# Two attention layers on one core: v from seven block products instead of eight

## The chip, the core and the metric

The kernel runs on one core of a Trainium2 chip. A core has a matrix engine (TensorE, "PE" in the profile, with its weight loads as "PEld"), a vector engine (VectorE, "DVE"), a scalar engine (ScalarE, "ACT"), GpSimd ("POOL") and SyncE ("SP"). POOL and SP here mostly issue DMAs. TensorE writes only to PSUM, and VectorE and ScalarE take the results out. The metric is the device time of one execution in microseconds (us).

## The reference

The input x has 16 batches of 256 channels by 32 x 32 positions. Two layers are applied, each `x = x + attention(norm(x))`. Cut to what matters, a layer is:

```python
def layer(x):                                 # x: (16, 256, 32, 32)
    xf = group_norm(x, G=16).reshape(16, 256, 1024)
    q, k, v = (einsum('oc,bcn->bon', Wt, xf) + bt[None, :, None] for Wt, bt in ...)
    q, k, v = (y.reshape(16, 4, 64, 1024) for y in (q, k, v))     # 4 heads
    sim  = einsum('bhdi,bhdj->bhij', q, k)
    qpos = einsum('hdi,bhdj->bhij', (rel_h + rel_w), q)
    attn = softmax(sim + qpos, axis=-1)
    out  = einsum('bhdn,bhmn->bhdm', v, attn)
    return x + out.reshape(x.shape)
```

All data are float32. The normalisation takes its groups over the last axis, two columns of the 32 to a group. What the change touches is v: for each batch and layer, a 1024 x 256 matrix of tokens times a 256 x 256 weight.

## The kernel before

A **unit** is one batch in one layer. There are 32 units, in an order that puts units of layer 0 and of layer 1 beside each other (`units`). A unit has four **blocks**, (pr, half): pr is the pair of heads (0 or 1), half is the half of the 1024 query positions. They are called b0 to b3 here; n is the number of a block over all units, and `block(n)` writes it out. In a block:

- There are eight tiles of scores, j = 0 to 7, of 128 keys by two heads by 512 queries. `seed` (line 344) has VectorE write the position term into two banks of PSUM; `scores` (line 373) has TensorE add k times q, and ScalarE takes the exponential into a buffer p of the pool `ppool` (12 buffers).
- `add_up` (line 397) sums the p tiles on VectorE. The eighth is added by an accumulating DMA from POOL (`add_last`, line 435), and the sum over keys is folded by further DMAs from POOL and SP (`fold`, `stack_up`, `fold_again`, `fold_stack`, `spread_sums`). `reciprocals` (line 508) makes the denominators, and `finish` (line 551) multiplies by them and adds the residual, two VectorE operations for a pair of blocks, and for layer 1 a store on SP.
- `attend` (line 409) multiplies v by p on TensorE, in two halves; `take_out` copies the result with ScalarE.

TensorE works on four quarters of its array, 64 x 64 each. A product over 128 rows needs two of them, which add into the same bank, so every product is made in two halves (`stretches`, line 157; `BANKS`): in the first half each row half of the array has a bank of its own, in the second they change over. The second half may start when the first has ended. A small write on POOL, the token (`word`, line 164), carries this from TensorE to TensorE.

Between the score tiles of a block stand products for the next blocks (`prepare`, line 593): in b0 the second half of the tokens' v and q of the second pair; in b1 k and the position term of that pair; in b2 q and k of the next unit's first pair; in b3 the first half of the next unit's v, and its position term. `values` (line 286) makes v for 512 tokens: 32 matmuls of 256 columns. `norms` lays the group sums, squares and the application of the normalisation for later units over the blocks, on ScalarE (tables `APPLY`, `SUMS`, `SQUARES`).

PSUM has eight banks, used as four buffers of two (`ring`). Three serve the score tiles in turn; they and the fourth also serve the products above and the result of `attend`. A buffer can be written again when the copy or the exponential that reads it is done. The program runs under a manual schedule: each engine and each queue executes its instructions in the order in which the code above makes them, and the order within `block` is written by hand.

Of the kernel before, what the change touches and what calls it, by code (L numbers as in the profile page):

```python
# [9 lines left out]
F32 = mybir.dt.float32  # L10
F32R = mybir.dt.float32r
I32 = mybir.dt.int32
AF = mybir.ActivationFunctionType
ALU = mybir.AluOpType
# [3 lines left out]
P = 128  # L18
HALF = 512
G = 16  # L20
# [32 lines left out]
def fast_path(ctx, tc, sh, x, layers, out, W, den_all, token, good, flag):  # L53
# [36 lines left out]
    small = ctx.enter_context(tc.tile_pool(name="small", bufs=2))  # L90
    kqpool = ctx.enter_context(tc.tile_pool(name="kqpool", bufs=2))
    vpool = ctx.enter_context(tc.tile_pool(name="vpool", bufs=2))
    ppool = ctx.enter_context(tc.tile_pool(name="ppool", bufs=12))
    apool = ctx.enter_context(tc.tile_pool(name="apool", bufs=3))
    spool = ctx.enter_context(tc.tile_pool(name="spool", bufs=2))
    fpool = ctx.enter_context(tc.tile_pool(name="fpool", bufs=2))
# [52 lines left out]
    def psum2(tag, name):  # L149
        return ps_s.tile([P, 2, HALF], F32, tag=tag, name=name)  # L150
# [6 lines left out]
    def stretches(products):  # L157

        done = []

        def word():
            if len(done) == 1:
                done.append(nc.gpsimd.memset(token, 0.0).ins)  # L166
                tc.add_manual_dep(done[1], done[0].name, SYNC, reason="first stretch done")

        def of(t):
            if t == 1:  # L170
                word()
            for ins in products(t):
                if t == 0:
                    done[:] = [ins.ins]
                elif len(done) == 2:
                    tc.add_manual_dep(ins.ins, done.pop().name, SYNC, reason="second stretch")

        of.word = word
        return of
# [106 lines left out]
    def values(u, g, pv):  # L286
# [24 lines left out]

        return stretches(products), out_of_psum

    def positions(u, pr, pa):

        l = units[u][1]
        pa = pa.rearrange("p h (e r) -> p h e r", r=D)

        def products(t):
            if t == 1:  # L320
                return
            for j in range(NT):
                for rs, h in BANKS[0]:
                    for x, c in enumerate(QUARTERS):
                        j0 = j * P + x * D
                        yield nc.tensor.matmul(  # L326
                            pa[c, h, j, :],
                            qs[u, pr][rs, j0 : j0 + D],
                            W.rel[l][rs, pr, :],
                            start=(j == 0),  # L330
                            stop=(j == NT - 1),
                            skip_group_check=True,
                        )

        def out_of_psum():
            abt[u, pr] = kqpool.tile([P, 2, NT, D], F32, tag="abt", name=f"abt_{u}_{pr}")
            nc.scalar.copy(abt[u, pr], pa)

        return stretches(products), out_of_psum
# [33 lines left out]
    def scores(blk, j, tag=None):  # L373
# [20 lines left out]
        nc.scalar.activation(p, ps, AF.Exp, bias=W.shift)  # L394
        probs[blk, j] = p

    def add_up(blk, j):
        u, pr, half = blk
        if j == 0:
            return  # L400
        if j == 1:
            accs[blk] = apool.tile([P, 2, HALF], F32, tag="acc", name=f"acc_{u}_{pr}_{half}")
            nc.vector.tensor_tensor(accs[blk], probs[blk, 0], probs[blk, 1], ALU.add)  # L403
        else:
            nc.vector.tensor_tensor(accs[blk], accs[blk], probs[blk, j], ALU.add)  # L405
# [3 lines left out]
    def attend(blk, po):  # L409

        u, pr, half = blk

        def products(t):
            for j in range(NT):
                p = probs[blk, j]
                for rs, a in BANKS[t]:
                    for h, c in enumerate(QUARTERS):
                        c0 = pr * P + h * D
                        yield nc.tensor.matmul(  # L419
                            po[c, a, :QUART],  # L420
                            vts[u][rs, j, c0 : c0 + D],
                            p[rs, h, a * QUART : (a + 1) * QUART],
                            start=(t == 0 and j == 0),
                            stop=(t == 1 and j == NT - 1),
                            skip_group_check=True,
                        )

        return stretches(products)
# [20 lines left out]
    def stack_up(blk):  # L449

        u, pr, x = blk
        if x == 0:
            stacks[u, pr] = spool.tile([P, HALF], F32, tag="stack", name=f"stack_{u}_{pr}")
        for h, at in beside(blk):
            nc.sync.dma_start(at, accs[blk][:R, h, :])
# [108 lines left out]

    def in_range(den, i):

        t = fpool.tile([P, den.shape[-1]], F32, tag=f"range{i}", name=f"range{i}", bufs=1)
        yield nc.vector.tensor_scalar(t, den, DEN_LO, None, ALU.is_ge)
        yield nc.vector.scalar_tensor_tensor(t, den, DEN_HI, t, ALU.is_le, ALU.mult)
        yield nc.vector.tensor_reduce(good[:, i : i + 1], t, AX.X, ALU.min)  # L570
# [22 lines left out]
    def prepare(u, b):  # L593

        x, y = ring[3], ring[2]
        if b == 0:
            return (
                values(u, 1, psum2(x, f"pv_{u}_1")),
                project(u, 1, "q", psum2(y, f"pq_{u}_1")),
            )  # L600
        if b == 1:
            return (
                project(u, 1, "k", psum2(x, f"pk_{u}_1")),
                positions(u, 1, psum2(y, f"pa_{u}_1")),
            )
        u += 1
        if u == NU:
            return (nothing, nothing), (nothing, nothing)
        if b == 2:
            return (  # L610
                project(u, 0, "q", psum2(x, f"pq_{u}_0")),
                project(u, 0, "k", psum2(y, f"pk_{u}_0")),
            )
        return (
            values(u, 0, psum2(x, f"pv_{u}_0")),
            positions(u, 0, psum2(y, f"pa_{u}_0")),
        )


    APPLY = {0: (0, 1, 5, 9, 9), 1: (9, 9, 9, 11, G)}  # L620
    SUMS = {0: (0, 0, 0, 2, 9), 1: (9, 11, 12, G, G)}
    SQUARES = {2: (0, 0, 5, 11, G)}

    FIRST_SQUARES = {0: (3, 5, 9, G, G)}
# [15 lines left out]
    def block(n):  # L640
# [3 lines left out]

        stacked = blocks[n - 3][:2] if half == 1 and n > 2 else None
        summed = blocks[n - 4][:2] if half == 0 and n > 3 else None
        before = blocks[n - 5][:2] if half == 1 and n > 4 else None
        after = blocks[n + 1] if n + 1 < len(blocks) else None
        previous = blocks[n - 1] if n > 0 else None
        one, two = u + 1 < NU, u + 2 < NU  # L650
# [5 lines left out]
        folded = n - 1 < FOLDED  # L656
        if not pieces:
            return block_without_pieces(n, half)

        if previous:  # L660
            if half == 0:
                add_up(previous, 5)
            add_up(previous, 6)
            if folded:
                add_last(previous)
            else:
                add_up(previous, 7)
# [15 lines left out]
        first.word()  # L683
        if half == 0:
            second.word()
        if stacked:
            fold_stack(*stacked, D)
        if summed:
# [9 lines left out]
        scores(blk, 5)  # L698
        if previous and folded:
            stack_up(previous)  # L700
        add_up(blk, 2)
        if n == 0:
            reduced(2, 0)
# [18 lines left out]
        values_of_p = attend(blk, po)  # L722
        values_of_p(0)
        if two and half == 1:
            if b == 1:
                mean_out = norm_mean(u + 2, filled(f1, f"pm_{n}", 0.0))
            else:
                mean_out = norm_var(u + 2, filled(f1, f"pm_{n}", EPS / 2))
        if after:
            scores(after, 0)  # L730
        if n == 0:
            mean_out = norm_var(1, filled(f1, f"pm_{n}", EPS / 2))
        values_of_p.word()
        if stacked:
            fold_stack(*stacked, R // 2)
        if previous and folded:
# [2 lines left out]
            load_x(units[u + 3][0], range(pr_, pr_ + 1) if u > 0 else range(CC))  # L739
        if half == 0 or n == len(blocks) - 3:  # L740
            add_up(blk, 5)
        if before:
            finish(*before)
        if two and half == 1 or n == 0:
# [9 lines left out]
        if summed:  # L754
            reciprocals(*summed)
        norms(u, b, 3)
        values_of_p(1)
        take_out(blk, po)
        pos[n] = po
# [399 lines left out]
class Weights:  # L1159


    def __init__(self, tc, sh, layers, const):
        nc = tc.nc
        self.sh, self.layers = sh, layers

        def new(name, shape):
            return const.tile(shape, F32, tag=name, name=name)

        self.ident = new("ident", [P, P])
        make_identity(nc, self.ident)  # L1170
        self.avg, self.ones = new("avg", [P, P]), new("ones", [P, P])
        self.mhalf, self.shift = new("mhalf", [P, sh.H]), new("shift", [P, 1])
        for t, v in (
            (self.avg, 1.0 / sh.COUNT),
            (self.ones, 1.0),
            (self.mhalf, -0.5),
            (self.shift, -SHIFT),
        ):
            nc.vector.memset(t, v)
        both = range(len(layers))  # L1180
        self.wq, self.wk, self.wv = (
            [new(f"{n}{l}", [P, sh.CC, sh.C]) for l in both] for n in ("Wq", "Wk", "Wv")
        )
        self.bq, self.bk, self.bv = (
            [new(f"{n}{l}", [P, sh.CC]) for l in both] for n in ("bq", "bk", "bv")
        )

        self.rel = [new(f"rel{l}", [P, sh.CC, sh.D]) for l in both]

    def load_rest(self, queue, l):  # L1190

# [70 lines left out]
```

## Time and profile before

| what | value |
|---|---|
| median of 3 runs | 2531.03 us (2530.86 to 2531.93) |
| span of the profiled execution | 2529.2 us |
| TensorE busy | 2508.5 us, 99% |
| VectorE busy | 2270.3 us, 90% |
| ScalarE busy | 1945.5 us, 77% |
| GpSimd busy | 836.1 us, 33% |
| granted clock of TensorE, mean | 0.999 |
| DMA queue of POOL / of SP, share of 16 DMA engines | 31.5% / 11.9% |

The times below come from the one profiled execution. Lines of groups read: source line, engine, operation, output <- inputs by the program's names, shapes, count, then busy us and mean ns of one. A line of the timeline reads: start (us from the start of the span), duration (us), engine, source line, operation, tiles, shape, count, and in brackets how long the engine stood idle before it and whose end it waited for. A line of the chain reads: start, duration, engine, tile, line, count. A float32 matmul stands as two instructions in the trace, so x8 is four matmuls, one for each quarter of the array. The end of a matmul in the profile is modelled and overlaps the start of the next, so stretches of TensorE are measured here from start to start.

### The profile page before, as it was taken

Reading aid. Unit: us, or ns where it says so; the run is one execution under the profiler, and the core shown is the slowest. Engines: PE = TensorE matmul, PEld = TensorE weight load, DVE = VectorE, ACT = ScalarE, POOL = GpSimd, SP = SyncE. Lnnn points to the kernel's source line nnn. Section 1 sums busy time; section 2 is a strip of 40 time slices with the busy share of each in tenths; the row PEclk is TensorE's granted clock in tenths of the full one; section 3 lists DMA queues with packets and bytes.
Section 4 is the critical chain, followed back from the end, with each engine's and each line's share of the span. In section 5 each row is a group of like instructions: output and inputs, shape, how many; then the busy total and the mean of one; then the engine's idle time right before and its main releaser. Section 6 shows DMA issues by size and latency. Waiting matters only on the chain.

```text
span 2529.2 us, 85968 instructions
## 1 busy us (share of the span) xinstructions
PE 2508.5 (99%) x37472; PEld 1331.3 (53%) x37472; DVE 2270.3 (90%) x2143; ACT 1945.5 (77%) x3855; POOL 836.1 (33%) x1196
## 2 busy tenths in 40 slices
PE   8999999999999999999999999999999999999998
PEld 4555555555555555555555555555555555555554
DVE  7898998999989989999899899998998999989998
ACT  6778777788777787777877778877778777787754
POOL 1332333323333333333233332333323333323320
PEclk9999999999999999999999999999999999999999
DMA  3344444444445444444444444454454444444442
GB/s 93 75 81 83 77 87 76 95 95 93 99 88 103 80 84 93 90 83 96 94 85 95 81 97 80 84 106 88 89 111 82 87 81 84 78 83 80 95 82 70
DMA packets 119841, 221.58 MB, mean 88 GB/s; under 512 B 53912, under 2 KB 55448, under 8 KB 119456
## 3 DMA queue, kind: packets, MB, share of 16 engines
q0 software_dynamic: 53712, 130.10, 31.5%
q1 hardware_dynamic: 65744, 85.90, 11.9%
q8 instruction: 295, 4.83, 0.8%
q14 instruction: 90, 0.74, 0.1%
HBM read 51.78 MB, written 17.30 MB: 27 GB/s over the span
## 4 chain that ended last, share of the span: by engine, by line
PE 96%; DVE 2%; DMA 1%; issue 1%; POOL 0%; SPq 0%; ACT 0%; DVEq 0%; POOLq 0%
PE po L419 34%; PE ps L385 34%; PE pv L298 9%; PE pk L268 9%; PE pq L268 9%; PE pa L326 2%; DVE ps L349 1%; DVE acc L405 0%; PE pm L209 0%; DMA den_all<-d 0%; DMA stack<-stack 0%; DMA x<-in_x_dram 0%; DVE acc L403 0%; PE raw_t L126 0%; POOL rstd L237 0%
## 5 line engine op out<-in xcount | busy, mean ns | idle before, releaser
L349 DVE TENSOR_TENSOR ps<-abt 128x1024 f32<-128x1024 f32 x1018 | 1229.2, 1230 | 227.0 <-ACT p L394 142.9
L394 ACT ACTIVATE p<-ps,shift 128x1024 f32<-128x1024 f32 x1024 | 1091.3, 1114 | 332.6 <-PE ps L385 332.6
L385 PE MATMUL ps<-q,k 64*64 64x512 f32 x8192 | 986.2, 590 | 1.3 <-DVE ps L349 1.2
L419 PE MATMUL po<-p,v 64*64 64x256 f32 x16384 | 930.6, 376 | 0.0
L419 PEld LDWEIGHTS po<-p,v 64*64 64x64 f32 x16384 | 629.6, 133 | 363.1 <-issue 77.2
L405 DVE TENSOR_TENSOR acc<-acc,p 128x1024 f32<-128x1024 f32 x643 | 780.6, 1214 | 7.0
L385 PEld LDWEIGHTS ps<-q,k 64*64 64x64 f32 x8192 | 306.7, 133 | 397.8 <-issue 272.9
L166 POOL MEMSET token<- 1x1 f32 x320 | 36.4, 114 | 1042.8 <-PE po L419 463.2
L465 POOL DMA_DIRECT2D stack<-stack x310 | 254.9, 822 | 189.5 <-DMA stack<-stack 103.6
L298 PE MATMUL pv<-Wv,xn 64*64 64x256 f32 x4096 | 244.3, 376 | 0.4 <-POOL token L166 0.3
L268 PE MATMUL pk<-xn,Wk 64*64 64x512 f32 x2048 | 242.9, 590 | 0.0
L268 PE MATMUL pq<-xn,Wq 64*64 64x512 f32 x2048 | 242.9, 589 | 0.0
L460 POOL DMA_DIRECT2D stack<-acc x248 | 221.8, 1079 | 40.2 <-issue 31.7
L248 ACT ACTIVATE xn<-x,nshift,rstd 128x128 f32<-128x128 f32 x496 | 210.4, 497 | 1.1 <-POOL nshift L239 1.1
L298 PEld LDWEIGHTS pv<-Wv,xn 64*64 64x64 f32 x4096 | 153.8, 133 | 102.7 <-issue 51.5
L436 POOL DMA_DIRECT2D acc<-p x124 | 118.9, 958 | 247.6 <-ACT od L480 159.4
L190 ACT ACTIVATE junk<-x,neg 128x128 f32<-128x128 f32 x505 | 197.7, 400 | 0.0
L480 ACT COPY od<-po 128x512 f32<-128x512 f32 x127 | 74.3, 585 | 116.9 <-PE po L419 116.9
L403 DVE TENSOR_TENSOR acc<-p,p 128x1024 f32<-128x1024 f32 x128 | 155.8, 1217 | 0.0
L441 POOL DMA_DIRECT2D acc<-acc x124 | 105.9, 854 | 148.2 <-DMA acc<-p 137.9
L268 PEld LDWEIGHTS pq<-xn,Wq 64*64 64x64 f32 x2048 | 78.3, 133 | 141.0 <-issue 132.5
L190 ACT ACTIVATE junk<-x 128x128 f32<-128x128 f32 x464 | 140.6, 313 | 0.0
(78 smaller groups left out, 1122.9 us busy)
## 6 DMA issues: line engine op xcount, KB each, us to landing
acc<-p POOLq DMA_DIRECT2D x124, 512.0 KB, 5.7
rden<-rd SPq DMA_DIRECT2D x126, 256.0 KB, 5.8
acc<-acc POOLq DMA_DIRECT2D x124, 256.0 KB, 3.5
x<-in_x_dram SPq DMA_DIRECT2D x32, 512.0 KB, 3.9
stack<-acc SPq DMA_DIRECT2D x248, 64.0 KB, 2.1
stack<-acc POOLq DMA_DIRECT2D x248, 64.0 KB, 2.9
out_dram<-x SPq DMA_DIRECT2D x31, 512.0 KB, 3.7
stack<-stack POOLq DMA_DIRECT2D x62, 128.0 KB, 4.0
```

Of the source, the lines that this page charges most:

```text
L190: nc.scalar.activation(junk, grouped(xt[units[u][0]], g), func, accum_out=into[:, g : g + 1], **bias)
L248: nc.scalar.activation(grouped(xns[u], g), grouped(xt[units[u][0]], g), AF.Identity, bias=shift[:, g : g + 1], scale=rstd[:, g : g + 1],)
L268: yield nc.tensor.matmul(pk[c, nh, :], w[l][rs, cc, c0 : c0 + D], xns[u][rs, cc, nh * HALF : (nh + 1) * HALF], start=(t == 0 and cc == 0), ...
L298: yield nc.tensor.matmul(pv[c, a, i, :], xns[u][rs, cc, j0 : j0 + D], W.wv[l][rs, cc, :], start=(t == 0 and cc == 0 and i == 0), stop=(t = ...
L349: nc.vector.tensor_tensor(ps.rearrange("p h (w y) -> p h w y", y=H), ab[:, :, :H].unsqueeze(2).to_broadcast([P, 2, XH, H]), ab[:, :, H + h ...
L385: nc.tensor.matmul(ps[c, h, :], a[hs, j0 : j0 + D], b[hs, columns], start=bool(tag) and i == 0, stop=i == len(terms) - 1, skip_group_check ...
L394: nc.scalar.activation(p, ps, AF.Exp, bias=W.shift)
L403: nc.vector.tensor_tensor(accs[blk], probs[blk, 0], probs[blk, 1], ALU.add)
L405: nc.vector.tensor_tensor(accs[blk], accs[blk], probs[blk, j], ALU.add)
L419: yield nc.tensor.matmul(po[c, a, :QUART], vts[u][rs, j, c0 : c0 + D], p[rs, h, a * QUART : (a + 1) * QUART], start=(t == 0 and j == 0), s ...
L460: nc.gpsimd.dma_start(at, acc[R:D, h, :], accum_op=ALU.add)
L465: nc.gpsimd.dma_start(stack[:rows_], stack[rows_ : 2 * rows_], accum_op=ALU.add)
```

## The change

v of the next unit is no longer made with eight products of blocks (128 channels by 128 channels by 512 tokens) in b3 and b0, but with seven, all in b3, for all units but the first.

- **Sums of the inputs.** The 256 channels x 1024 tokens of the normalised x are four quarters. Three sums of them are made by DMA into a tile t: SP copies a quarter twice (`sum_copies`), POOL adds two quarters (`sum_additions`), SP copies a sum twice, POOL adds twice more. The copies and two of the additions stand in b2, the third addition in b3. `Weights.mix` makes the four sums of the weights, once per layer, on VectorE.
- **Products.** `Values.half` makes one row half of a product with eight matmuls of 128 columns; `stage` interleaves two such halves on different quarters of the array. Product 1 is paired with score tile 2, which is cut into 128 columns for it (`score_half`, `exponential`); products 6 and 2, 5 and 7, 3 and 4 make pairs. Bank 0 of the buffer `pw` holds a running sum that ScalarE copies into v four times (`keep`); bank 1 holds a second one that VectorE adds to or takes from v four times (`combine`). A pair that writes a bank waits for the keep or combine that reads it.
- **Order of the blocks.** `block_with_values` writes out b3, `block_with_q` b0 (from the second unit on), in which only q is left between score tiles: half of it ahead of tile 4, half after tile 5. `attend` in b3 is cut so that pair 4 stands within its first half. The addition of tile 5 moves from the end of b0 to the start of b1. The first pair's `finish` moves from b1 to b2, and the tables of `norms` are shifted a little.
- **Buffers.** `ppool` goes from 12 to 10 buffers, which makes room for t; a range check near the end takes a buffer of that pool.

```diff
-    ppool = ctx.enter_context(tc.tile_pool(name="ppool", bufs=12))
+    ppool = ctx.enter_context(tc.tile_pool(name="ppool", bufs=10))
+    tpool = ctx.enter_context(tc.tile_pool(name="tpool", bufs=1))
...
+        into, of = (t[:, 2:4, :], t[:, 0:1, :]) if second else (t[:, 0:2, :], x[:, 1:2, :])
+        nc.sync.dma_start(into, of.to_broadcast([P, 2, HALF]))
...
+        into, of = (
+            (t[:, 0:2, :], x[:, 0:4:3, :]),
+            (t[:, 2:4, :], x[:, 3:4, :].to_broadcast([P, 2, HALF])),
+            (t[:, 3, :], x[:, 2, :]),
+        )[i]
+        nc.gpsimd.dma_start(into, of, accum_op=ALU.add)
...
+        def half(self, i, rs, whole):
+            a, x, w, first = self.terms[i]
+            for part in range(4):
+                for q, c in enumerate(QUARTERS):
+                    j0 = part * P + q * D
+                    yield nc.tensor.matmul(
+                        self.pw[c, a, part * P : (part + 1) * P],
+                        x[rs, j0 : j0 + D],
+                        w[rs, :],
...
+            for _ in range(4):
+                for g in streams:
+                    for _ in range(2):
+                        made.append(next(g))
...
+        def keep(self, oc, nh, sign):
+            nc.scalar.activation(
+                self.out(oc, nh), by_token(self.pw[:, 0, :]), AF.Copy, scale=sign
+            )
+        def combine(self, oc, nh, op):
+            o = self.out(oc, nh)
+            nc.vector.tensor_tensor(o, o, by_token(self.pw[:, 1, :]), op)
...
-    SUMS = {0: (0, 0, 0, 2, 9), 1: (9, 11, 12, G, G)}
+    SUMS = {0: (0, 0, 0, 1, 7), 1: (7, 9, 11, G, G)}
...
+        if b == 2:
+            sum_copies(u + 1, False)
         if previous:
-            if half == 0:
+            if half == 0 or u > 0:
                 add_up(previous, 5)
...
+    def block_with_q(n):
...
+        for j in range(1, 4):
+            scores(blk, j)
+        first, first_out = project(u, 1, "q", psum2(r3, f"pq_{u}_1"))
+        first(0)
+        norms(u, 0, 0)
+        seed(blk, 4, r1)
+        scores(blk, 4)
+        add_up(blk, 1)
+        norms(u, 0, 1)
+        seed(blk, 5, r0)
+        scores(blk, 5)
+        first.word()
...
+        first(1)
+        first_out()
+        seed(blk, 6, r2)
+        scores(blk, 6)
...
+    def block_with_values(n):
...
+        add_up(previous, 6)
+        scores(blk, 1)
+        one = v.half(1, HI, False), v.half(1, LO, True)
+        two_halves = score_half(blk, 2, 0), score_half(blk, 2, 1)
+        v.stage("1", (two_halves[0], two_halves[1]), (one[0], one[1]), 0)
+        v.word("1")
+        add_last(previous)
+        scores(blk, 3)
+        v.stage("1", (two_halves[0], two_halves[1]), (one[0], one[1]), 1)
+        v.keep(0, 0, 1.0)
+        exponential(blk, 2)
+        ab, ab_out = positions(u + 1, 0, psum2(r1, f"pa_{u + 1}_0"))
+        ab(0)
+        ab_out()
+        v.pair("2", 6, 2, 0)
+        v.word("2")
+        sum_additions(u + 1, 2)
+        seed(blk, 4, r0)
+        scores(blk, 4)
+        add_up(blk, 1)
+        v.pair("2", 6, 2, 1)
+        v.keep(1, 0, 1.0)
+        seed(blk, 5, r2)
+        scores(blk, 5)
+        seed(blk, 6, r1)
+        scores(blk, 6)
+        v.combine(0, 0, ALU.add)
+        fold_stack(*stacked, D)
+        fold(previous)
+        v.pair("3", 5, 7, 0)
+        v.word("3")
+        seed(blk, 7, r0)
+        scores(blk, 7)
+        v.pair("3", 5, 7, 1)
+        v.keep(1, 1, -1.0)
...
+        add_up(blk, 2)
+        add_up(blk, 3)
+        seed(after, 0, r1)
...
+        v.combine(1, 1, ALU.subtract)
+        po = psum2(r2, f"po_{n}")
+        values_of_p = attend(blk, po)
+        values_of_p(0, range(NT // 2))
+        v.pair("4", 3, 4, 0)
+        v.word("4")
...
+        values_of_p(0, range(NT // 2, NT))
+        scores(after, 0)
+        values_of_p.word()
+        v.pair("4", 3, 4, 1)
+        v.keep(0, 1, -1.0)
...
+        add_up(blk, 4)
...
+        if before:
+            finish(*before)
+        v.combine(1, 0, ALU.add)
```

## The prediction

> **What bounds the kernel now.** I read the busy shares first, then the chain that ended last.
>
> ```profile
> span 2529.2 us, 85968 instructions
> ...
> PE 2508.5 (99%) x37472; PEld 1331.3 (53%) x37472; DVE 2270.3 (90%) x2143; ACT 1945.5 (77%) x3855; POOL 836.1 (33%) x1196
> ...
> PE 96%; DVE 2%; DMA 1%; issue 1%; POOL 0%; SPq 0%; ACT 0%; DVEq 0%; POOLq 0%
> ```
>
> TensorE is never out of work: 96% of the chain is its own. VectorE has only 10% to spare, so what it is given matters. Next the chain in order of time, and the timeline of TensorE, in one unit (b0 to b3 are its four blocks).
>
> ```profile
> 1275.95 1.73 PE pv L298 x32
> ...
> 1299.18 0.93 PE pa L326 x64
> ...
> 1335.51 1.73 PE pv L298 x32
> ```
>
> ```profile
> 1293.85 2.75 PE L385 MATMUL ps<-q,k 64*64 64x512 f32 x24
> ...
> 1312.11 2.75 PE L385 MATMUL ps<-q,k 64*64 64x512 f32 x24
> ...
> 1332.75 2.76 PE L385 MATMUL ps<-q,k 64*64 64x512 f32 x24
> ...
> 1351.03 2.75 PE L385 MATMUL ps<-q,k 64*64 64x512 f32 x24
> ```
>
> The starts of the blocks: b0 at 1273.19, then these four. So b0 takes 20.66, b1 18.26, b2 20.64, b3 18.28, a unit 77.84 us. The chain's stretches are v 1.725 each (four a unit), a score tile 0.858, q or k 1.72 a half, the values product 3.45 a half, positions 0.93; their sum fills the unit. Any new wait of TensorE therefore lengthens the kernel by its whole size. What feeds the score tiles is the cycle seed (VectorE), scores, exponential (ScalarE); b1 shows it in the VectorE timeline:
>
> ```profile
> 1296.11 1.23 DVE L349 TENSOR_TENSOR ps<-abt 128x1024 f32<-128x1024 f32 x1 [1.85 <-ACT p L394]
> 1297.25 1.22 DVE L403 TENSOR_TENSOR acc<-p,p 128x1024 f32<-128x1024 f32 x1
> 1298.38 1.23 DVE L349 TENSOR_TENSOR ps<-abt 128x1024 f32<-128x1024 f32 x1
> ```
>
> VectorE had nothing else to do and still had to wait for the first exponential; its fourth seed starts 2.26 us into the block (1296.11 less 1293.85), and the fifth ends at 1299.61, 5.76 us into it. An operation of 1.22 follows the last after 1.14. In b1 of before nothing suffers: k's two halves and the positions stand ahead of score tile 5. What a late seed costs shows at the kernel's head:
>
> ```profile
> 20.96 2.36 DVE L349 TENSOR_TENSOR ps<-abt 128x1024 f32<-128x1024 f32 x2
> ...
> 22.24 1.09 PE L385 MATMUL ps<-q,k 64*64 64x512 f32 x8 [1.25 <-DVE ps L349]
> ```
>
> The first of the two seeds ends at about 20.96 + 1.23 = 22.19; TensorE starts 0.05 later, and the tile takes 1.09 where the others take 1.04. A wait thus costs 0.10 beyond the seed's end.
>
> **The change, part by part.**
>
> *The products of v.* Removed: 4 x 1.725 = 6.90 us a unit. Added: 7 products of 16 matmuls of 128 columns, 28 rounds of four array quarters; and score tile 2 of b3, cut the same way, 4 rounds for its 0.858. A round of 512 columns takes 0.429 x 2 = 0.858 (scores), of 256 takes 1.725/4 = 0.431, of 64 takes 0.93/8 = 0.116. Per column that is 1.676, 1.68 and 1.81 ns; 128 columns lie between 0.2145 and 0.232, by the slope between the two neighbours 0.2205 (0.116 + 64 x (0.431 - 0.116)/192 = 0.221). So v costs 28 x 0.2205 = 6.17, the cut tile 0.88: a gain of 0.70 us a unit, 22 us over 31 units. A rule speaks against it. The Trainium skill (TensorE: Matmul & The Clock Gate, Back-to-back issue gap) puts a stream of weight load and matmul pairs at 128 columns at about 81 ns a pair against 56 for the stream alone, 25 ns more. With 256 instructions on four quarters, 64 in a row, that is 1.6 us a unit: the gain would be a loss of 0.9. The positions row has pairs with half as many columns, in the same quarter order, and loses 9 ns a round against 0.107 at the rate of the long rows, not 25 ns for each of two passes; I take the row.
>
> *b0 (block_with_q).* It loses v's second half (3.45): 17.21 us. But q alone now stands between the score tiles. VectorE's order there is seed 4, first addition, seed 5, as in the b1 lines, from the same first exponential: seed 5 ends at 5.76, and TensorE can go on at 5.86. It gets there after tiles 1 to 3, half of q and tile 4: 3 x 0.858 + 1.72 + 0.858 = 5.15. In before, v's and q's second and first halves, 3.4 us, stood in between. **Stall 0.71.** Seed 5 cannot be earlier by VectorE being ahead, since it hangs on the exponential of tile 1; behind it in TensorE's queue stand everything else of the block and the next. The q copy (ScalarE: exponential 4 from 5.40, four applications at 0.39, exponential 5, q) ends at about 10.09 and frees the bank of the values product when TensorE arrives at 10.16: 0.03.
>
> *b3 (block_with_values).* Work: 18.28 - 3.45 + 6.17 + 0.03 = 21.03. Counted from its start, with an exponential beginning 0.25 after TensorE has left its tile (1293.85 + 0.86 + 0.25 = 1294.96, the row of ScalarE):
> Tile 1, half of (tile 2, product 1), tile 3, the other half: 3.48; positions to 4.41. ScalarE: exponential 3 from 2.85, the first keep after it, 3.86 to 4.45 (128x512 from PSUM: the od copy, 585 ns). Pair 2 overwrites what keep reads, so it starts at about 4.55: stall 0.14. Behind keep wait exponential 2 (to 5.46) and the positions' copy (to 6.4).
> VectorE: seed 4 needs exponential 3, 3.96, so 4.00; from there it runs without a break at 1.14: addition 1 at 5.14, seed 5 at 6.28, seed 6 at 7.42, combine at 8.56 (0.60 if 128x512 takes the 0.69 of the multiplication out of PSUM at L561 less the same 0.09 overlap), seed 7 at 9.16, additions 2 and 3, the next block's seed 0, combine 2 from 13.72 to 14.41.
> TensorE: pair 2's halves and tile 4 to 7.17; tile 5 needs seed 5 (7.51 + 0.10 = 7.60): stall 0.43. Tile 6 needs seed 6 (8.65 + 0.10): 0.28. Pair 3, tile 7, pair 3, half of the values: 13.94, no stall. Pair 4 overwrites the bank that combine 2 reads: 14.50, stall 0.56. The rest 7.87, to 22.4. **Stalls 1.41.** The bounds: 0.4 if VectorE issues closer and keep is early, 2.2 if a combine takes 1.0 us.
>
> *VectorE's whole load.* Four combines 2.4 us a unit on 70.9 (2270.3/32): 73.3 of 79, no bound on the average. The residual of the first pair moves from b1 to b2 with its store on SP, two operations, 2.36: in b2 VectorE stood 0.43 and 1.85 us before seeds (1330.69, 1335.00), and seed 1 of b3 is still early; cost nothing, and if that cover were gone 31 x up to 0.5. The addition of tile 5 that moves from b0 to b1 fits b1's wait of 1.85, and the eight operations on weights are two groups in all.
>
> *ScalarE.* Four keeps at 0.585 replace two v copies at 1.01; the moved group sums (0.3 each) lie in its waits. Twelve to ten p buffers: exponential j now reuses what tile j-2 of the last block held, whose last reader is the addition at the start of this one, done before; nothing.
>
> *DMAs and the POOL and SP queues.* Rows for the two kinds:
>
> ```profile
> acc<-p POOLq DMA_DIRECT2D x124, 512.0 KB, 5.7
> ...
> x<-in_x_dram SPq DMA_DIRECT2D x32, 512.0 KB, 3.9
> ```
>
> From b2's start: copy 1 lands at 4.0; addition 1 follows the token of k (1319.31, 7.2 in), lands at 13.0; copy 2, behind four spreads and two stack copies on SP, lands at 17.2; addition 2 lands at 23.0, 2.35 into b3. Pair 2 wants it at 4.55: hidden with 2.1 us to spare, and each us beyond costs 31. On POOL, addition 2 holds back two stack additions and b3's first token to about 20, wanted at 22.4. Reciprocals, behind SP's wait for copy 2, have until late b3. Addition 3 (5.8 to 10) is wanted at 13.9. The accumulating queue goes from 31.5% to some 41% of the DMA engines.
>
> *Sum.* A unit becomes 17.21 + 0.74 + 18.26 + 20.64 + 21.03 + 1.41 = 79.29, 1.45 more; x 31 = 45 us on the profiled 2529.2, so 2574; the median stands 1.8 above the span: **2576 us**.
>
> **The rivals.** *Faster:* the seeds aren't late. This needs less than 0.70 us of stalls a unit; none gives 2531 - 22 = 2509. For it: VectorE has idle time in each block of before. Against: that idle time is spent waiting for the very exponential on which seed 5 hangs, and b0's stall alone is 0.71. *No change:* b3 is mild and b0's stall pays off the gain, 2531. *The sums land late:* four transfers in a row with added traffic; 1 to 2 us past the slack, 31 to 62 more, 2607 to 2638. For it: the whole chain has 2.1 us over 23. Against: DMA is 40% busy. *Short matmuls cost what the rule says:* 1.6 us a unit more, of which some 0.7 fall into the stalls: 2576 + 28 = 2604.
>
> **How the numbers follow.** Stalls as counted 0.60 (own range 2553 to 2600, from 1.4 to 2.9 us of stalls a unit), late sums 0.17, dear matmuls 0.08, no change 0.05, faster 0.10. A measurement of this kernel tells 0.2% from no change, 5 us. Slower 0.85, same 0.05, faster 0.10. The range from 2533 to 2615 leaves out the faster case and the worse half of the late sums.
>
> **What would show it.** Right: about 31 idle spells of TensorE of 0.7 us ahead of tile 5 in b0, released by the seed; three of 0.3 to 0.6 in b3, two by seeds and one by a combine; the cut matmuls at 0.22 a round; units near 79.3. Wrong: b0 at 17.2 without a stall, b3 near 21, waits on a DMA ahead of pair 2, or rounds of 0.25 and more.

## The result, and the profile after

The changed kernel takes **2690.55 us** (median of 4 runs, 2682.01 to 2693.86) against 2531.48 (2530.86 to 2532.01) for the kernel before: a ratio of 1.0623, 95% interval 1.0605 to 1.0642. It is slower, as forecast, but by 159 us instead of 45, and outside the range of 2533 to 2615. Its profiled execution has 2682.0 us, a span of 2680.2. It also scatters more than before, 12 us against 1.2.

The head of the page and the shares of the chain that ended last, after:

```profile
span 2680.2 us, 94366 instructions
PE 2536.3 (95%) x41192; PEld 1394.9 (52%) x41192; DVE 2343.8 (87%) x2244; ACT 1959.7 (73%) x3917; POOL 936.5 (35%) x1351
...
PE 62%; DVE 17%; issue 11%; DMA 7%; ACT 2%; POOL 1%; DVEq 0%; SPq 0%; POOLq 0%
```

TensorE was 96% of the chain and is now 62%. VectorE and the DMAs have taken shares of it, and TensorE's share of the span has fallen from 99% to 95%. Next the timeline of TensorE through one unit, after; only rows that begin a block, and those that stand around a wait.

```profile
1308.84 2.75 PE L493 MATMUL ps<-q,k 64*64 64x512 f32 x24
...
1329.48 1.04 PE L493 MATMUL ps<-q,k 64*64 64x512 f32 x8
...
1334.47 0.33 PE L513 MATMUL ps<-q,k 64*64 64x128 f32 x2 [2.16 <-POOL token L396]
...
1338.19 0.33 PE L368 MATMUL pw<-mixed,t 64*64 64x128 f32 x2 [1.68 <-ACT abt L445]
...
1344.71 1.08 PE L368 MATMUL pw<-mixed,t 64*64 64x128 f32 x32
1345.58 1.94 PE L548 MATMUL po<-p,v 64*64 64x256 f32 x32
...
1355.81 2.75 PE L493 MATMUL ps<-q,k 64*64 64x512 f32 x24
...
1362.31 1.09 PE L493 MATMUL ps<-q,k 64*64 64x512 f32 x8 [1.17 <-DVE ps L457]
...
1374.42 2.75 PE L493 MATMUL ps<-q,k 64*64 64x512 f32 x24
```

b2 starts at 1308.84, b3 at 1329.48, b0 at 1355.81, b1 at 1374.42. In b3 TensorE waits twice for what POOL and its DMAs make: for the first token (1334.47), and before 1338.19, where pair 2 starts, for the input sum that it reads. The row puts that second wait down to the positions' copy (ScalarE), which ended just then, at 1338.17. But pair 2 does not need that copy: in no_sums, a run below that leaves the sums out, pair 2 starts 0.8 us before the copy does. The sum in `t` landed at 1338.05, and in 29 of the 31 units pair 2 starts 0.13 to 0.14 us after this landing. In b0 TensorE waits for seed 5, 1.17 us by the row.

The lengths of the blocks, each from its score tile 1 to the next block's (tile 0 is made at the end of the block before), beside the forecast. They are means over the units of one profiled execution, for b0 from the second unit on:

| | b0 | b1 | b2 | b3 | unit |
|---|---|---|---|---|---|
| before | 20.69 | 18.27 | 20.55 | 18.27 | 77.78 |
| forecast | 17.95 | 18.26 | 20.64 | 22.44 | 79.29 |
| after | 18.62 | 18.31 | 20.55 | 25.16 (23.26 to 28.30) | 82.64 |

4.86 us more a unit, x 31 = 151 us, is the whole difference of the two spans (2680.2 - 2529.2 = 151.0). Against the forecast b3 is 2.72 us too long and b0 0.67, together 105 us of the 106 between the spans' forecast (2574) and 2680.2.

Now the chain behind b3's two waits, in the same unit: POOL's timeline, then SP's, after. The sums are made in the order copy 1 (SP), addition 1 (POOL), copy 2 (SP), additions 2 and 3 (POOL); pair 2 reads what addition 2 makes.

```profile
1316.59 1.23 POOL L336 DMA_DIRECT2D t<-xn  x1 [0.47 <-ACT junk L191]
1317.33 1.37 POOL L594 DMA_DIRECT2D stack<-stack  x1
...
1331.40 1.23 POOL L336 DMA_DIRECT2D t<-xn  x1 [5.82 <-DMA t<-t]
1332.13 2.25 POOL L589 DMA_DIRECT2D stack<-acc  x2
1333.18 1.24 POOL L396 MEMSET token<- 1x1 f32 x1
1333.21 2.10 POOL L565 DMA_DIRECT2D acc<-p  x1
```

```profile
1308.73 0.66 SPq L327 DMA_DIRECT2D t<-xn  x1
1322.09 2.44 SPq L602 DMA_DIRECT2D den_all<-stack  x4
1324.63 1.18 SPq L584 DMA_DIRECT2D stack<-acc  x2
1325.90 0.65 SPq L327 DMA_DIRECT2D t<-t  x1
```

Read together: addition 1 is issued at 1316.59 and has landed at 1321.77. The fold of the sums over keys that is issued behind it (1317.33) lands at 1322.07, and only then may SP issue the four spreads that read it; these and two stack copies occupy SP for 3.81 us, and copy 2 is issued at 1325.90. It lands at 1331.12. POOL, which has stood in addition 2 for 5.82 us, issues it at 1331.40, and behind it two stack additions and the first token, for which TensorE has been ready since about 1332.2. Addition 2 lands at 1338.05, 8.6 us into b3. This is no matter of one unit; the list of waits of after (total us, times, longest):

```profile
POOL t L336 <- DMA t<-t: 148.7, 31, 6.5
...
PEld ps L513 <- POOL token L396: 63.1, 31, 3.8
...
PE pw L368 <- DMA t<-xn: 18.4, 26, 2.0
```

POOL stands before addition 2 in every one of 31 units. From start to start, the first token holds TensorE up by 1.4 us in the mean (0.1 in no_sums).

### The profile page after: what moved, and what is told of

The parts are those of the page before. It is cut to its first block, busy times and chain, and to the rows that moved or that the text cites. A ratio compares the mean times of both kernels' runs of the same rounds, so it can differ in the third digit from the quotient of the medians.

```text
span 2680.2 us, 94366 instructions
## 1 busy us (share of the span) xinstructions
PE 2536.3 (95%) x41192; PEld 1394.9 (52%) x41192; DVE 2343.8 (87%) x2244; ACT 1959.7 (73%) x3917; POOL 936.5 (35%) x1351
## 3 DMA queue, kind: packets, MB, share of 16 engines
q0 software_dynamic: 75040, 170.74, 38.5%
q1 hardware_dynamic: 82608, 118.41, 14.4%
## 4 chain that ended last, share of the span: by engine, by line
PE 62%; DVE 17%; issue 11%; DMA 7%; ACT 2%; POOL 1%; DVEq 0%; SPq 0%; POOLq 0%
PE po L548 21%; PE ps L493 21%; PE pk L269 8%; DVE ps L457 8%; PE pq L269 6%; DMA t<-xn 4%; DVE acc L534 4%; PE pw L368 4%; DVE v L420 2%; DVE acc L532 1%; DVE od L659 1%; ACT v L414 1%; PE pa L434 1%; DMA acc<-p 1%; DMA stack<-acc 1%
## 5 line engine op out<-in xcount | busy, mean ns | idle before, releaser
L502 ACT ACTIVATE p<-ps,shift 128x1024 f32<-128x1024 f32 x993 | 1067.3, 1113 | 455.6 <-PE ps L493 305.5
L493 PE MATMUL ps<-q,k 64*64 64x512 f32 x7944 | 981.3, 592 | 42.6 <-DVE ps L457 38.5
L493 PEld LDWEIGHTS ps<-q,k 64*64 64x64 f32 x7944 | 297.1, 133 | 427.7 <-issue 228.2
L594 POOL DMA_DIRECT2D stack<-stack x310 | 277.3, 894 | 164.0 <-DMA stack<-stack 100.2
L167 POOL MEMSET token<- 1x1 f32 x258 | 24.9, 96 | 735.6 <-PE po L548 438.2
L589 POOL DMA_DIRECT2D stack<-acc x248 | 238.0, 1200 | 36.0 <-DMA stack<-acc 19.0
L570 POOL DMA_DIRECT2D acc<-acc x124 | 129.0, 1040 | 226.3 <-DMA acc<-p 209.4
L565 POOL DMA_DIRECT2D acc<-p x124 | 136.7, 1102 | 200.1 <-ACT p L502 189.5
L368 PE MATMUL pw<-mixed,t 64*64 64x128 f32 x2976 | 141.9, 275 | 39.4 <-DMA t<-xn 18.4
L336 POOL DMA_DIRECT2D t<-xn x93 | 103.0, 1108 | 180.4 <-DMA t<-t 148.7
L368 PEld LDWEIGHTS pw<-mixed,t 64*64 64x64 f32 x2976 | 117.8, 134 | 92.8 <-POOL token L396 30.1
```

The lines of the kernel that those rows point to most:

```text
L368: yield nc.tensor.matmul(self.pw[c, a, part * P : (part + 1) * P], x[rs, j0 : j0 + D], w[rs, :], start=first and not whole and part == 0, ...
L493: nc.tensor.matmul(ps[c, h, :], a[hs, j0 : j0 + D], b[hs, columns], start=bool(tag) and i == 0, stop=i == len(terms) - 1, skip_group_check ...
L589: nc.gpsimd.dma_start(at, acc[R:D, h, :], accum_op=ALU.add)
L594: nc.gpsimd.dma_start(stack[:rows_], stack[rows_ : 2 * rows_], accum_op=ALU.add)
```

## The experiments

The theory at this point: b3 is long because the input sums come late through SP's and POOL's queues; b0 because seed 5 is late. Numbers of the combines in the expectations are those of the pairs they follow (combine 4 stands behind pair 4). The text ahead of the prediction, the prediction and one expectation count four combines a unit; there are three: the code calls `combine` three times, and the trace has 93 of them (L420), 3 x 31.

**copy2_first.** Only the place of copy 2 on SP is moved, to right behind addition 1.

```diff
         if b == 2:
             sum_additions(u + 1, 0)
+            sum_copies(u + 1, True)
...
-        if b == 2:
-            sum_copies(u + 1, True)
```

> Only the place of the second copy of the input sums on the SP queue is changed: it stands right behind the first addition, ahead of the four spreads and two stack copies of the block. Theory 1 (the queue: POOL stands in the second addition until this copy has landed, and the first token of b3 stands behind it): the copy starts about 5.2 us after the first addition is issued, some 4 us earlier than in the changed kernel; token and second addition are then on time, b3 falls from a mean of 25.16 to about 22.4 us, 31 x 2.7 = 85 us less, about 2605 us. Theory 2 (b3 is long because VectorE's chain of seeds and combines is slow): b3 stays near 25, time within 10 us of 2690.

**no_sums.** The input sums are left out, so that v is not what the reference asks; every product reads the plain quarters of x, with the same matmuls and tokens.

```diff
-            x, t = quarters_of_x(u), sums_x[u]
+            x = t = quarters_of_x(u)
...
-            sum_copies(u + 1, False)
+            pass
...
-            sum_additions(u + 1, 0)
...
-            sum_copies(u + 1, True)
...
-            sum_additions(u + 1, 1)
...
-        sum_additions(u + 1, 2)
```

> The input sums are left out: products 4 to 7 read plain quarters of x, so that v is not the reference's; copies and additions of b2 and b3 are gone, all else stands. Theory 1: b3 at the 22.4 us of the timetable (21.03 of work, 1.41 of waits for keep, seeds and combine), b0 at 18.6 as in the changed kernel, about 2606 us, and the same as the kernel with the copy moved. Theory 2: b3 near 25, 2690 us. Should the traffic itself be the cost, this one is well below the kernel with the copy moved.

Measured: copy2_first **2614.6** us, ratio 1.0328 (1.0298 to 1.0358); no_sums **2607.89**, 1.0301 (1.0271 to 1.0331). Blocks: copy2_first 18.61, 18.31, 20.55, 23.04; no_sums 18.64, 18.31, 20.57, 22.66. POOL's timeline of copy2_first, in a unit whose b3 starts at 1297.12:

```profile
1284.24 1.23 POOL L336 DMA_DIRECT2D t<-xn  x1 [0.47 <-ACT junk L191]
...
1293.61 1.23 POOL L336 DMA_DIRECT2D t<-xn  x1 [0.38 <-issue]
...
1299.23 0.09 POOL L396 MEMSET token<- 1x1 f32 x1 [0.35 <-PE pw L368]
```

Addition 2 is issued 9.4 us after addition 1 instead of 14.8, and in this unit the token no longer waits for a queue but for TensorE itself (in four of the 31 it is still 0.9 to 2.1 us late). The place of one DMA issue on SP is worth 76 us. All the traffic of the sums that is left after that costs at most the 7 us between the two kernels, so the loss was waiting in a queue, not the bytes: POOL's queue goes from 31.5% to 38.5% of the DMA engines. Without the sums b3 has a median of 22.54 us; the prediction's timetable of it, made without late sums, said 22.44.

**q_before_5.** The rest of the loss includes b0. The second half of q is put ahead of score tile 5 and its seed.

```diff
-        seed(blk, 5, r0)
-        scores(blk, 5)
         first.word()
...
         first(1)
         first_out()
+        seed(blk, 5, r0)
+        scores(blk, 5)
```

> Only b0 is changed: the second half of q stands ahead of score tile 5, not behind it. If b0's 18.61 us hold 1.4 us of waiting for seed 5 (b0 ends at 5.15 + 1.72 us where seed 5 is ready by 6.5), b0 falls to about 17.25, 31 x 1.36 = 42 us less, 2648 us. If VectorE is behind as a whole rather than at this one seed, the wait moves to tiles 6 and 7 or into b1 and less than half of it is won, 2670 us or more.

Measured: **2690.29** us, 1.0627 (1.0596 to 1.0658), b0 18.59: nothing gained. TensorE's timeline of q_before_5, tiles 5 and 6 and then tile 7 of one b0:

```profile
1274.30 1.90 PE L493 MATMUL ps<-q,k 64*64 64x512 f32 x16
1277.34 1.09 PE L493 MATMUL ps<-q,k 64*64 64x512 f32 x8 [1.14 <-DVE ps L457]
```

Tile 5 no longer waits, but tiles 5 to 7 now take 3.94 us, start to start, where their work is 2.57. The wait has moved two tiles back, to tile 7. So what bounds b0 is not one seed but VectorE's run from seed 4 to seed 7 with the additions in between.

**early_and_q.** Both together, and addition 1 with copy 2 moved further up, ahead of b2's first two tokens.

```diff
+            sum_additions(u + 1, 0)
+            sum_copies(u + 1, True)
         first.word()
...
         first(1)
         first_out()
+        seed(blk, 5, r0)
+        scores(blk, 5)
```

> Three moves: the second copy ahead of the spreads, the first addition ahead of the two tokens of b2 on POOL (some 3 us earlier again), and q's second half ahead of tile 5 in b0. If the causes are separate they add: 2690 - 85 - 42 = 2563 us with b0 17.25, b1 18.26, b2 20.64, b3 22.4. If TensorE's lost time in b3 is what kept VectorE's lag small, b0 and b1 get longer and the time stays above 2580.

Measured: **2607.94** us, 1.0302 (1.0272 to 1.0331), as much as no_sums to 0.1 us. The sums are now as good as free, and q's place again gives nothing (b0 18.59): the two causes did not add up to the 2563 that was expected.

Why is seed 5 late by 1.35 us (tile 5 at 1362.31 where TensorE got there at about 1360.96) and not by 0.71? VectorE's timeline of copy2_first, at the end of b3 and in the b0 that starts at 1320.19:

```profile
1311.44 0.69 DVE L420 TENSOR_TENSOR v<-v,pw 128x512 f32<-128x512 f32 x1 [0.37 <-ACT v L414]
...
1313.51 0.19 DVE L236 TENSOR_REDUCE var<-pm 128x16 f32<-128x32 f32 x1 [0.18 <-PE pm L210]
...
1317.75 0.69 DVE L420 TENSOR_TENSOR v<-v,pw 128x512 f32<-128x512 f32 x1 [0.34 <-ACT v L414]
1318.47 2.37 DVE L457 TENSOR_TENSOR ps<-abt 128x1024 f32<-128x1024 f32 x2
1320.75 2.47 DVE L534 TENSOR_TENSOR acc<-acc,p 128x1024 f32<-128x1024 f32 x2
1323.15 1.23 DVE L457 TENSOR_TENSOR ps<-abt 128x1024 f32<-128x1024 f32 x1
```

Between 1311 and 1323 VectorE's only idle time is 0.9 us, lost ahead of two combines that wait for a keep and of the group variance. It enters b0 with the rest of a seed and two additions still to do, and seed 4 starts 2.96 us into the block (1323.15 - 1320.19), not 2.26. At 2.26, as in b1 of before, the exponential would have set it; at 2.96 it is VectorE's own backlog. This backlog is not new. VectorE's timeline of before, in the b0 that starts at 1273.19:

```profile
1273.73 2.47 DVE L405 TENSOR_TENSOR acc<-acc,p 128x1024 f32<-128x1024 f32 x2
1276.12 1.25 DVE L349 TENSOR_TENSOR ps<-abt 128x1024 f32<-128x1024 f32 x1
...
1278.42 1.22 DVE L349 TENSOR_TENSOR ps<-abt 128x1024 f32<-128x1024 f32 x1
```

There too seed 4 stands behind two additions of the previous block and starts 2.93 us in, without a wait, and seed 5 ends at 6.45 (over the units 2.92 and 6.44, after 2.95 and 6.45). It did no harm, because v and q stood ahead of tile 5. Three runs try to remove it.

**combine4_first.** On copy2_first: the last combine is put ahead of the keep of the same pair, so that VectorE need not wait for ScalarE.

```diff
-            v.pair("4", 3, 4, 1)
-            v.keep(0, 1, -1.0)
...
+            v.pair("4", 3, 4, 1)
             v.combine(1, 0, ALU.add)
+            v.keep(0, 1, -1.0)
```

> Built on the kernel with the copy moved (copy2_first, 2614.6 us, b0 18.61, b3 mean 23.04). The last pair's combine is written ahead of the last keep, so that VectorE's combine waits for TensorE and no longer for ScalarE's keep; TensorE, ScalarE and VectorE run the same operations in the same order. Theory (b0 is 0.66 us longer than forecast because this combine, and with it two seeds, two additions and seed 4, come 0.6 to 0.7 us late): b0 falls to about 18.0, 31 x 0.6 = 19 us less, about 2596. Rival (b0 is long because VectorE has too much work between two exponentials): b0 stays at 18.6 and the time at 2614.

**order_b0.** On early_and_q: in b0 the seeds go ahead of the additions; `add_last` and the next block's seed 0 move along with them.

```diff
+        add_up(previous, 5)
         seed(blk, 4, r1)
         scores(blk, 4)
-        add_up(blk, 1)
+        add_up(previous, 6)
...
         seed(blk, 7, r1)
         scores(blk, 7)
+        add_up(blk, 1)
+        add_up(blk, 2)
```

> Built on early_and_q (2607.9 us; b0 18.58). In b0 alone VectorE's order is changed: seed 4 behind one addition of the previous block instead of two, seeds 5, 6 and 7 ahead of this block's additions 1 and 2; the same operations. Theory (b0 is bound by VectorE's run from seed 4 to seed 7, which holds two additions of 1.14 us): b0 falls to its TensorE work of 17.2, 31 x 1.35 = 42 us less, 2566 us. Rival (VectorE's total in b0 and b3 is the bound): the lag comes back in b1, b1 rises from 18.26 and at most half is won, 2587 or more.

**order_both.** order_b0, combine4_first, and in b3 two additions moved.

```diff
         add_last(previous)
+        add_up(blk, 1)
...
         seed(blk, 4, r0)
         scores(blk, 4)
-        add_up(blk, 1)
...
-        add_up(blk, 3)
...
+        add_up(blk, 3)
         values_of_p(0, range(NT // 2, NT))
```

> order_b0 with VectorE's order changed in b3 too: addition 1 in the wait ahead of seed 4, additions 2 and 3 behind the seed and the combine that TensorE waits for, and the last combine ahead of the last keep. By the timetable b3 keeps 0.14 us for the first keep, 0.1 at pair 3, 0.2 at tile 7 and 0.05 at pair 4: 21.5 us; b0 17.25. Unit 20.64 + 18.26 + 21.5 + 17.25 = 77.65 against 77.84 before: 2525 us, a little faster than before. If VectorE's 19.9 us in b3 and 16.1 in b0 cannot be laid beside TensorE's 38.2, b0 or b1 grow and the time stays above 2545.

combine4_first: **2627.41** us, 1.0377 (1.0356 to 1.0397), 13 us slower than copy2_first, with b0 at 18.80, which is 6 us of the 13. The theory that this one wait makes b0 long fell, as the rows of before, which have no combine, would have told. VectorE's timeline and then ScalarE's, combine4_first, at the end of b3:

```profile
1320.41 0.68 DVE L420 TENSOR_TENSOR v<-v,pw 128x512 f32<-128x512 f32 x1
1321.76 2.37 DVE L457 TENSOR_TENSOR ps<-abt 128x1024 f32<-128x1024 f32 x2 [0.66 <-ACT v L414]
```

```profile
1321.13 0.60 ACT L414 ACTIVATE v<-pw 128x512 f32<-128x512 f32 x1 [0.82 <-DVE v L420]
```

VectorE reached the combine only when it was done with `finish`, so the keep now waited for the combine, and the seed that writes the same buffer for the keep. The wait was turned round, not removed.

order_b0: **2572.82** us, 1.0161 (1.0141 to 1.0181), blocks 17.21, 18.45, 20.66, 22.76. VectorE's timeline in a b0 that starts at 1295.16:

```profile
1297.41 1.23 DVE L457 TENSOR_TENSOR ps<-abt 128x1024 f32<-128x1024 f32 x1 [0.48 <-ACT p L502]
1298.55 1.22 DVE L534 TENSOR_TENSOR acc<-acc,p 128x1024 f32<-128x1024 f32 x1
1299.69 3.50 DVE L457 TENSOR_TENSOR ps<-abt 128x1024 f32<-128x1024 f32 x3
```

Seed 4 stands 2.25 us into the block and waits for the exponential; seeds 5 to 7 follow one another. b0 takes 17.21 us, which is TensorE's work and no stall. The order of VectorE's work was worth 35 us here (2607.94 - 2572.82).

order_both: **2572.12** us, 1.016 (1.0143 to 1.0177), blocks 17.47, 18.83, 20.56, 22.15, and not the 2525 expected. b3 gained 0.6 and b0 and b1 lost as much. In b3 the commonest length is 21.67 (12 of 31 units), but in some units the third token is late, as in POOL's timeline of order_both in a b3 from 1271.29:

```profile
1274.19 0.87 POOL L565 DMA_DIRECT2D acc<-p  x1 [0.70 <-DVE acc L534]
...
1283.13 0.82 POOL L570 DMA_DIRECT2D acc<-acc  x1 [3.82 <-PE ps L493]
1283.67 0.32 POOL L396 MEMSET token<- 1x1 f32 x1
```

The fold at 1283.13 reads what the addition of 1274.19 makes, which landed at 1282.61, 8.4 us after its issue; the token stands behind the fold. (The row puts the wait down to TensorE.)

**order_all.** order_b0's and order_both's order without combine4_first, with the fold behind the third token, addition 2 ahead of b2's token of the values, the next unit's seed 3 ahead of the last combine, and one addition later in b1.

```diff
-        fold(previous)
         v.pair("3", 5, 7, 0)
         v.word("3")
+        fold(previous)
...
+        seed(after, 3, r1)
         v.combine(1, 0, ALU.add)
-        seed(after, 3, r1)
```

> order_both (2572.1 us; means b0 17.47, b1 18.83, b2 20.56, b3 22.15) with five moves and the same work: the second addition of the sums ahead of b2's last token on POOL, fold of the previous block behind token 3 in b3, the last keep again ahead of the last combine, seed 3 of the next block ahead of that combine, and in b1 addition 2 behind seed 7. If what is left of b3 above 21.6 is late sums and token 3, and what is left of b0 and b1 above 17.2 and 18.3 is late seeds: unit 20.64 + 18.3 + 21.5 + 17.25 = 77.7, 2526 to 2535 us, as before. If VectorE has no more room (94% by the count of the forecast), the waits come back at other tiles and it stays above 2550.

**order_all_nc.** order_all with the combines of VectorE left out, so that v lacks what they add.

```diff
-        v.combine(0, 0, ALU.add)
...
-        v.combine(1, 1, ALU.subtract)
...
-        v.combine(1, 0, ALU.add)
```

> order_all with VectorE's four combines left out, so that v lacks the terms in bank 1; TensorE, ScalarE and the DMAs do all they did. 2.4 us a unit less on VectorE and no pair waits for a combine. If VectorE's share is what is left between order_all and the 22 us of gain by the products, b3 is 21.1 to 21.3, b0 17.2, b1 18.26, b2 20.64, unit 77.3, about 2515 us, below before. If something else holds it (tokens, sums, keeps), it stays within 5 us of order_all.

Measured: order_all **2574.73** us, 1.0163 (1.0149 to 1.0177), blocks 17.81, 18.74, 20.58, 22.07: not better than order_b0, and far from the 2526 to 2535 expected. What b3 saved came back as waits of 0.4 to 0.6 us in b0 (tile 3) and in b1 (group sums). order_all_nc **2552.68**, 1.008 (1.0061 to 1.0098), blocks 17.26, 18.80, 20.62, 21.62. The page's engine rows, order_all and then order_all_nc:

```profile
PE 2521.9 (98%) x41192; PEld 1539.5 (60%) x41192; DVE 2352.3 (91%) x2244; ACT 1953.4 (76%) x3917; POOL 938.8 (36%) x1351
```

```profile
PE 2508.8 (98%) x41192; PEld 1559.2 (61%) x41192; DVE 2288.2 (90%) x2151; ACT 1952.1 (77%) x3917; POOL 944.4 (37%) x1351
```

VectorE does 64 us less, 93 combines of 0.69, and the kernel is 22 us faster, between the two cases of the expectation. What the combines cost on VectorE is thus as large as what the products were forecast to gain on TensorE (0.70 x 31 = 22). Even so it stays 20 us above before: b0 and b3 together are then 0.08 us shorter than before, but b1 is 0.53 longer, where the group sums wait as in order_all. No version that was run is as fast as the kernel before. That no order of this scheme could be faster was not shown; only these were tried.

## Why the prediction was wrong, point by point

The direction was not luck: no_sums, without the late sums, is 76 us slower than before, by the stalls that were forecast: those of b3 as counted, that of b0 larger. What failed is one link in the path of the sums and, second in size, the place of b0's seed 4.

- **Products and short matmuls: right.** The second half of pair 3, four rounds, runs from 1344.71 to 1345.58, 0.2175 us a round; the forecast was 0.2205. The rule that I weighed against it (the Trainium skill, TensorE: Matmul & The Clock Gate, Back-to-back issue gap) would have made it 0.2205 + 1.6/32 = 0.27, by the estimate made from its figures (28 rounds of products and 4 of the cut tile). Here the row decides, and the rival of dear matmuls falls.
- **b1, b2: right** (18.31 and 20.55 against 18.26 and 20.64). The residual that moves to b2 and the addition that moves to b1 cost nothing, as said. (Of the two waits that were given as room in b2, the one at 1335.00 stands in b3, which starts at 1332.75.)
- **b3's own stalls: right.** With the sums out of the way (no_sums) the block's median is 22.54, its mean 22.66, against 22.44. The seeds and the combine stall TensorE as counted: in a unit of no_sums pair 2, tile 5 and pair 4 start 4.55, 7.60 and 14.59 us into b3, where the timetable has 4.55, 7.60 and 14.50.
- **The failed step** is in the paragraph on DMAs and queues: "copy 2, behind four spreads and two stack copies on SP, lands at 17.2" and from it "hidden with 2.1 us to spare". The first link was right: addition 1 landed 12.9 us after b2's start, forecast 13.0. With the 4.0 taken for a copy, 17.2 means that copy 2 is issued at 13.2, right behind addition 1, and the six small DMAs ahead of it cost nothing. It was issued at 17.06 in the unit shown (17.5 by the median of all units), because these six take SP 3.8 us and start only at 13.25. In before they run earlier, in a b2 that starts at 1312.11:

```profile
1319.77 0.81 POOL L465 DMA_DIRECT2D stack<-stack  x1 [0.37 <-issue]
```

```profile
1321.98 2.43 SPq L473 DMA_DIRECT2D den_all<-stack  x4
1324.53 1.16 SPq L455 DMA_DIRECT2D stack<-acc  x2
```

  There they start 9.87 us into the block and are over at 13.58 (14.0 by the median). At that place they would have made copy 2 only 0.4 to 0.8 us later than taken, an estimate from these rows. What the forecast left out is that addition 1 stands on POOL ahead of the fold that the spreads read. The fold is issued 0.8 us later and takes 4.7 us to land instead of 2.2 (medians of all units), so the six DMAs, which wait for the fold, in effect wait for addition 1 too. no_sums, which has no additions, bears this out: there the fold takes 2.2 us again, and the six start 9.88 us into a b2 that starts at 1271.05:

```profile
1280.93 3.28 SPq L602 DMA_DIRECT2D den_all<-stack  x4
1284.33 1.16 SPq L584 DMA_DIRECT2D stack<-acc  x2
```

  The later links were no longer than taken, by the median: copy 2 took 3.2 us to land (4.0 taken), addition 2 5.6 (5.8 taken); in the unit shown they took 5.2 and 6.65. So addition 2 landed 27.1 us after b2's start instead of 23.0 (29.2 in the unit shown), that is 6.4 into b3 where it is wanted at 4.55. "Addition 2 holds back two stack additions and b3's first token to about 20" moved with it: in the unit shown TensorE had the token at 25.6. The two waits are one delay, for TensorE spends the first part of it at the token. Pair 2 starts 6.82 us into b3 in the mean, against 4.58 in no_sums; that is 2.24 of the 2.50 us by which b3 is longer than there (25.16 - 22.66, x 31 = 78 us). The medians of the times put the whole term at 83 us (2690.55 - 2607.89), and copy2_first wins back 76 of it by the place of one issue. Addition 1 behind the fold on POOL, the other way to break this link, was not run.
- **The rival "the sums land late"** named what happened, "waits on a DMA ahead of pair 2" among the signs, but not its size: it gave 31 to 62 us where the sums cost 78 to 83. Its reason, "four transfers in a row with added traffic", falls short too: early_and_q has all of this traffic and stands at no_sums' time, so what counted was the place in the queues. With b0's 21 us on top the time left even this rival's range.
- **b0, second in size: the mechanism was right, the term too small.** "Stall 0.71" was 1.35 in the unit looked at, and b0 is 18.62 against 17.95, 21 us in all. The forecast read seeds 4 and 5 from the b1 lines, "from the same first exponential". But b1 of before has one addition of the previous block ahead of seed 4, while b0 has two and comes right behind `finish`: b0's own rows in before had seed 4 at 2.93 and seed 5 at 6.45, not 2.26 and 5.76. With 6.45 + 0.10 the forecast's own sum gives a stall of 1.40 and a b0 of 18.6. This backlog needs no combines, since before has none. order_b0 shows the cause: with one addition ahead of seed 4 and the others behind the seeds the stall is gone. q_before_5 shows that it was the run of VectorE and not tile 5's place.
- Combines were counted as four; they are three, so their load is about 1.9 us a unit (three, one every 0.64), not 2.4. The count went into the average load alone, not into a stall.
- What remains of b0 18.64, b3 22.66 and the rest in no_sums against the forecast is 32 us of the median: 21 by b0, 7 by b3; the last 4, in b1 and at the ends, were not looked into.

## What to carry to other kernels

A DMA that is moved onto a queue is late by the issue time of everything ahead of it there, and by what these wait for; it also holds up what stands behind it, and whatever waits for that on another queue. Read both from the queues' own timelines, item by item, before a transfer is called hidden. On a kernel whose fullest engine has no idle time, the second fullest is judged by its order in each block, read from that very block, and not by its average or from a block that looks alike. And when a wait is to be removed by changing two readers' order, first see when the second engine gets there: combine4_first turned it round and won nothing.

## What the runs showed of the hardware that I had not expected

- Small DMAs cost SP about 0.6 us each to issue: 2.44 us for four of 2 KB, 1.18 for two of 64 KB, in both kernels.
- DMAs of POOL landed later where an accumulating one stood ahead of them in the queue. For `acc<-p`, 512 KB, the median is 5.7 us in before; right behind addition 2 and two stack additions it took 9.4 (1333.21 to 1342.63). The 8 KB fold behind addition 1 took 4.75 (1317.33 to 1322.07); in before and in no_sums the same fold takes 2.2 by the median. The columns in the page's list of DMA issues are output, queue, count, KB and median us to landing; of after:

```profile
stack<-stack POOLq DMA_DIRECT2D x62, 8.0 KB, 4.7
```

- Putting 118.41 instead of 85.90 MB on SP's queue and 170.74 instead of 130.10 on POOL's cost next to nothing by itself: early_and_q moves all these bytes and stands at no_sums' time.
